# Four image layers on one Trainium2 core: the last layer's depthwise convolution of the first image on VectorE, its diagonals built later, its zeroing divided between two engines

## The chip, the cores and the metric

The program runs on one NeuronCore of a Trainium2 chip. TensorE (PE), VectorE (DVE), ScalarE (ACT), GpSimd (POOL) and SyncE (SP, which only starts DMAs here) each work through a queue of their own in order and wait for one another through semaphores. The metric is the device time of one execution, in microseconds (us). All data are float32.

## The reference

The reference passes 4 images of 192 channels and 56 x 56 pixels through four layers: a windowed attention, a channel gate, another windowed attention with a gated convolution, and a selective scan in four directions. Only the last layer is touched. Cut to what matters, with C = 192 channels, it is:

```python
xn = layer_norm_over_channels(x, ln_w, ln_b)
xc, z = split(in_proj_w @ xn)                       # 192 channels each
xc = silu(depthwise_conv3x3(xc, conv_w) + conv_b)   # 9 weights per channel
for k in range(4):           # rows, columns, and both backwards
    dts, Bv, Cv = split(x_proj_w[k] @ xs[k], [12, 16])
    dt = softplus(dt_proj_w[k] @ dts + dt_proj_b[k])
    h[t] = exp(dt[t] * A) * h[t - 1] + dt[t] * Bv[t] * xs[k][t]   # 4 states per channel
    ys[k][t] = sum(h[t] * Cv[t]) + Ds[k] * xs[k][t]
y = layer_norm_over_channels(sum of the four ys, out_norm_w, out_norm_b) * silu(z)
out = x + out_proj_w @ y
```

## The kernel before, in words

The 192 channels lie as two halves (h = 0, 1) of 96 partitions. Tiles that PE reads have 128 partitions; the 32 that hold no channel are set to zero once. An image has 3136 pixels, worked on in 7 chunks of 448, which are 8 rows of 56.

**Setup of the last layer (L1688 to L1754).** The weights come in by two DMAs (L219). Eight pairs of small matmuls (L1695) work out a projected bias into the PSUM tile `pb`, which DVE copies to `in_b` (L1702). DVE scales the projection weights `inT` by the norm's weights (L1704, one instruction per half) and finishes `a_neg` (L1707). `diag` holds 18 matrices of 96 x 96, one for each half and each of the 9 taps, each an identity times one tap's weight per channel; DVE makes them with 18 `tensor_scalar_mul` (L1722), after POOL has made the identity and zeroed the lower 32 partitions (L1719). The helper `keep` (L1727) allocates tiles and has POOL zero their lower partitions (L1732): two `u` and one `y` of 6272 columns, two `pad` of 1276, four `row` and two `sq` of 896. POOL also zeroes three `dr` (L1740).

**A chunk, `begin(b, c)` (L1792).** SP loads a row tile (L1803). POOL clears the pad's edge columns and copies two rows from the pad above (L1809 to L1815). Then the layer norm: PE averages over channels (L1768), DVE subtracts (L1770), ACT squares (L1778), PE averages (L1783), ACT takes logarithm and exponential (L1786, L1787), DVE multiplies (L1789). PE projects to the first 192 channels (L1821) and ACT writes them into the pad (L1832, one instruction per half). The convolution is on PE: for each half, 9 matmuls of a diagonal with a shifted view of the pad add up in one PSUM bank (L1851; a float32 matmul shows as two instructions), and ACT copies the bank to `u` with the bias (L1859). After each half PE projects one half of z (L1821), which ACT writes to a gate tile (L1868). ACT then applies SiLU to both (L1873, L1874), and `product` (L1887) multiplies `u` by the scan's weights (L1893) and stores the result in memory. When all 7 chunks are there, `begin_columns` does the same product over columns.

**Scans.** A step is one chunk in one direction, a half-step one half of it. It loads the products (`load`), makes dt (L1985, L1997), spreads it by DMA (L2023), takes exponentials (L2031), multiplies dt and u on DVE (L2046 or L2049), spreads this on PE (L2056), multiplies it on DVE (L2062), runs three scans on DVE (L2078), multiplies by C on POOL (L2085), sums on PE (L2101) and adds to `y` on DVE (L2106, L2111, L2115). `final` does the closing norm, the gate and the output projection.

**The order of the work.** `Order` (L241) is a planner that runs while the program is written. Each job is a generator that yields its next operation with an engine and an estimated duration, or a condition that must hold before it goes on. The planner always takes the operation with the smallest (estimated start + 0.05 us x place), and the engines' queues have that order on the chip. Jobs of image 0 have the places -52 + 6c for the chunks, and 2t + h for the scans. A job's next operation is not planned before the one before it has ended. A condition such as `gone("begun", ...)` only orders the plan; on the chip, only data that are written or read make an engine wait.

Of the kernel before, what the change touches and what calls it, by code (L numbers as in the profile page):

```python
# [13 lines left out]
AF = mybir.ActivationFunctionType  # L14
ALU = mybir.AluOpType
# [4 lines left out]
B, C, H, W = 4, 192, 56, 56  # L20
HW = H * W
HALF = 96
CH = 448
# [14 lines left out]
NS, DTR, SCH = 4, 12, 448  # L38
# [176 lines left out]
def load_packs(nc, pool, packs, aps):  # L215
    tiles = {}
    for name, pack in packs.items():
        t = pool.tile([pack.p, pack.n], F32, name=f"w_{name}")
        nc.sync.dma_start(t, aps[name])  # L219
        for n in pack.at:  # L220
            tiles[name + "." + n] = pack.view(t, n)
    return tiles


def pixels(ap):

    return ap.rearrange("(h p) n -> p h n", p=HALF)
# [9 lines left out]
def rows2(ap, w=W):  # L237
    return ap.rearrange("p (y x) -> p y x", x=w)


class Order:  # L241
# [25 lines left out]
    def done(self, tile):  # L267

        (slot,) = (s for slots in self.kinds.values() for s in slots if s[1] is tile)
        slot[0] = self.end + self.LATENCY  # L270
# [58 lines left out]
def on_dve(*n, takes=(), ready=None, each=0.00105):  # L329
    return "DVE", sum(0.08 + each * i for i in n), takes, None, ready  # L330
# [6 lines left out]
def on_act(*n, takes=(), table=None, ready=None):  # L337
    return "ACT", sum(0.2 + 0.0009 * i for i in n), takes, table, ready
# [6 lines left out]
def on_sp(*takes):  # L345
    return "SP", 0.5, takes, None, None
# [1329 lines left out]
def layer3(tc, src, packs, aps, dst):  # L1676
# [7 lines left out]
    nc = tc.nc  # L1684
    with ExitStack() as ctx:
        const = ctx.enter_context(tc.tile_pool(name="c_const", bufs=1))
        dram = ctx.enter_context(tc.tile_pool(name="c_dram", bufs=1, space=DRAM))
        w = load_packs(nc, const, packs, aps)  # L1688
# [25 lines left out]
        nc.vector.memset(eps, EPS)  # L1714

        ident = const.tile([HALF, HALF], F32, name="c_ident")
        make_identity(nc, ident)
        diag = const.tile([128, 2, 9, HALF], F32, name="diag")
        nc.gpsimd.memset(diag[HALF:], 0.0)  # L1719
        for h in range(2):  # L1720
            for t in range(9):
                nc.vector.tensor_scalar_mul(diag[:HALF, h, t], ident, w["c96.conv_w"][:, h, t : t + 1])  # L1722

        per = ctx.enter_context(tc.tile_pool(name="c_per", bufs=1))
        ps = ctx.enter_context(tc.tile_pool(name="c_ps", bufs=1, space=PSUM))

        def keep(name, shape, n, rows=128, zero=True):  # L1727

            tiles = [per.tile([rows, *shape], F32, name=f"{name}{i}") for i in range(n)]
            if zero:  # L1730
                for t in tiles:
                    nc.gpsimd.memset(t[HALF:], 0.0)  # L1732
            return tiles

        us = keep("u", [2, HW], 2)
        (y,) = keep("y", [2, HW], 1)
        pads = keep("pad", [2, 11, W + 2], 2)
        drs = keep("dr", [SCH], 3, zero=False)
        for t in drs:
            nc.gpsimd.memset(t, 0.0)  # L1740
        order = Order(
            nc,
            bank=[ps.tile([128, 512], F32, name=f"c_bank{i}") for i in range(8)],
            row=keep("row", [2, CH], 4),
            sq=keep("sq", [2, CH], 2),
            gate=keep("gate", [2, CH], 2, HALF, False),
            prod=keep("prod", [512], 2, 40, False),
            dr=drs,
            bc=keep("bc", [SCH], 8, zero=False),
            dt=keep("dt", [SCH], 6, HALF, False),  # L1750
            du=keep("du", [SCH], 3, HALF, False),
            da=keep("da", [SCH], 10, zero=False),
            st=keep("st", [SCH], 12, zero=False),
        )  # L1754
        take, done = order.take, order.done
        prods = [[dram.tile([40, HW], F32, name=f"prod{b}_{o}") for o in range(2)] for b in range(B)]
        zmem = [dram.tile([C, HW], F32, name=f"zmem{b}") for b in range(B)]
        passed = set()

        def gone(*what):  # L1760
            return what in passed
# [30 lines left out]
        def begin(b, c):  # L1792


            u = us[b % 2]

            yield lambda: (b, c) == (0, 0) or (gone("begun", b, c - 1) if c else gone("begun", b - 1, NCHUNK - 1))
            yield lambda: b < 2 or gone("scanned", b - 2)

            yield lambda: b == 0 or gone("multiplied", 8 * NSC * (b - 1) + 4 * c)  # L1800
            yield on_sp("row", "row")
            xl, xn = take("row"), take("row")
            nc.sync.dma_start(xl[:HALF], pixels(src[b])[:, :, c * CH : (c + 1) * CH])  # L1803

            i = NCHUNK * b + c
            pad, above = pads[i % 2], pads[(i - 1) % 2]
            yield lambda: i < 2 or gone("convolved", i - 2)
            yield on_pool(200, 200)
            nc.gpsimd.memset(pad[:HALF, :, :, 0 : W + 2 : W + 1], 0.0)  # L1809
            if c == 0:  # L1810
                nc.gpsimd.memset(pad[:HALF, :, 1], 0.0)
            else:
                nc.gpsimd.tensor_copy(pad[:HALF, :, 0:2, 1 : 1 + W], above[:HALF, :, 8:10, 1 : 1 + W])
            if c == NCHUNK - 1:
                nc.gpsimd.memset(pad[:HALF, :, 10], 0.0)  # L1815
            yield from layer_norm(xl, xn, over=(xl,))

            def project(m):
                px = take()
                for k in range(2):  # L1820
                    nc.tensor.matmul(  # L1821
                        px[:HALF, :CH], inT[:, k, HALF * m : HALF * m + HALF], xn[:, k], start=(k == 0), stop=(k == 1)
                    )
                return px

            tiles = []
            for m in range(2):
                yield on_pe(2 * CH, "bank")
                tiles.append(project(m))
            for m in range(2):  # L1830
                yield on_act(CH)
                nc.scalar.activation(  # L1832
                    pad[:HALF, m, 2:10, 1 : 1 + W],
                    rows2(tiles[m][:HALF, :CH]),
                    AF.Identity,
                    bias=in_b[:, m : m + 1],
                )
                done(tiles[m])
            passed.add(("begun", b, c))
            y0, y1 = max(8 * c - 1, 0), 8 * c + (8 if c == NCHUNK - 1 else 7)  # L1840
            n = y1 - y0
            at = y0 - (8 * c - 1)
            px = slice(y0 * W, y1 * W)
            zt = None
            for h in range(2):
                pz = pc = None
                for t in range(9):
                    yield on_pe(n * W, *(("bank",) if t == 0 else ()), ready=order.end - 0.5 if t else None)
                    if t == 0:
                        pc = take()  # L1850
                    nc.tensor.matmul(  # L1851
                        rows2(pc[:HALF, : n * W]),
                        diag[:, h, t],
                        pad[:, h, at + t // 3 : at + t // 3 + n, t % 3 : t % 3 + W],
                        start=(t == 0),
                        stop=(t == 8),
                    )
                yield on_act(n * W)
                nc.scalar.activation(  # L1859
                    u[:HALF, h, px], pc[:HALF, : n * W], AF.Identity, bias=w["c96.conv_b"][:, h : h + 1]  # L1860
                )
                done(pc)
                yield on_pe(2 * CH, "bank")
                pz = project(2 + h)
                yield on_act(CH, takes=() if h else ("gate",))
                if h == 0:
                    zt = take("gate")
                nc.scalar.activation(zt[:, h], pz[:HALF, :CH], AF.Identity, bias=in_b[:, 2 + h : 3 + h])  # L1868
                done(pz)
            done(xn)  # L1870
            passed.add(("convolved", i))
            yield on_act(2 * n * W, 2 * CH, table=SILU)
            nc.scalar.activation(u[:HALF, :, px], u[:HALF, :, px], AF.Silu)  # L1873
            nc.scalar.activation(zt, zt, AF.Silu)  # L1874
            yield on_sp()
            nc.sync.dma_start(pixels(zmem[b])[:, :, c * CH : (c + 1) * CH], zt)
            done(zt)
            yield from product(b, 0, px, u[:, :, px], 2)
            passed.add(("rows", b, c))

        def begin_columns(b, c):
            yield lambda: all(gone("rows", b, i) for i in range(NCHUNK))
# [242 lines left out]
        n = 8 * NSC  # L2125
        for b in range(B):
            for c in range(NCHUNK):
                order.add(n * (b - 1) + 6 * c + 4, begin(b, c))
                order.add(n * (b - 1) + 48 + c, begin_columns(b, c))
                order.add(n * (b + 1) - 2 * c, final(b, c))  # L2130
        for t in range(len(steps)):
            order.add(2 * t - 5, load(t))
            if t % 2 == 0:
                order.add(2 * t - 3, sizes((t, t + 1)))
            for h in range(2):
                order.add(2 * t + h - 1, decay(t, h))
                order.add(2 * t + h, scan(t, h))
# [35 lines left out]
```

## Time and profile before

| | us |
|---|---|
| median of 3 runs | 6957.4 (6956.57 to 6957.86) |
| profiled execution | 6951.71 |
| its span, first to last instruction | 6949.9 |
| PE busy | 5890.7 (85%) |
| DVE busy | 5908.5 (85%) |
| ACT busy | 2640.6 (38%) |
| POOL busy | 1423.8 (20%) |
| mean granted TensorE clock | 0.931 of full speed |

The last layer begins at about 4901 us. Its first real matmul starts at 4926.27 us, the pad of the first chunk is complete at 4943.0, that of the seventh at 5093.5. The first scan of image 0 starts at 5068.9, those of images 1, 2 and 3 at 5585.8, 6061.3 and 6528.2.

In timeline lines, the columns are the start, the time until the last of the merged instructions ends, engine, line, operation, output and inputs with their shapes, the count, and in brackets the idle time before with what ended it. A tile's or line's statistics give the shortest, median and longest duration in ns. An instruction that waits inside its engine for a port has the wait in its duration, not in the idle time before it.

### The profile page before, as it was taken

To read this page: it belongs to the slowest core of one execution; us is meant where nothing else is said; L and a number is where in the kernel's file an instruction comes from. 1 tells how busy PE (TensorE), PEld (TensorE's weight loads), DVE (VectorE), ACT (ScalarE), POOL (GpSimd) and SP (SyncE) were. 2 spreads that over 40 slices of the span, in tenths; PEclk is the share of its full clock that TensorE was granted. 3 is DMA by queue.
4 is the path that set the end of the run, shared out by engine and by line. 5 is a ranking of instruction groups with operands and counts; after the bars stand their busy time and mean duration, and the time that the engine had idled before them with its cause. 6 is when DMAs were issued, how large, how long until landed. Compare 5 with 4: busy or idle time off the path is not lost. (4 is left out here: it accounts for less than half of the span.)

```text
span 6949.9 us, 107660 instructions
## 1 busy us (share of the span) xinstructions
PE 5890.7 (85%) x43810; PEld 2685.0 (39%) x43810; DVE 5908.5 (85%) x7379; ACT 2640.6 (38%) x4083; POOL 1423.8 (20%) x1409
## 2 busy tenths in 40 slices
PE   4999979999999994968888787885799989899776
PEld 2445434444444441345444444442332222222211
DVE  2799999999999999648999898997348788887897
ACT  1111112221122211135555455543256656556543
POOL 0000000000000000032222222220125445445564
PEclk9999989999999997979999899987899999999998
DMA  3222112221222112110000000000145555555654
GB/s 94 56 52 64 34 35 53 58 65 35 52 64 61 35 45 73 45 52 16 19 19 14 19 17 17 19 14 8 34 104 130 142 143 129 152 133 136 166 151 108
DMA packets 252044, 462.69 MB, mean 67 GB/s; under 512 B 30388, under 2 KB 237964, under 8 KB 240412
## 3 DMA queue, kind: packets, MB, share of 16 engines
q1 hardware_dynamic: 251548, 455.80, 25.8%
q8 instruction: 345, 5.65, 0.3%
q14 instruction: 151, 1.24, 0.1%
HBM read 238.58 MB, written 62.96 MB: 43 GB/s over the span
## 5 line engine op out<-in xcount | busy, mean ns | idle before, releaser
L789 DVE TENSOR_TENSOR pr<-vdx,attn 112x1792 f32<-112x1792 f32 (+4 forms) x720 | 1185.6, 1648 | 19.0
L634 PE MATMUL a_bank<-qk_in,w_a 64*49 64x392 f32 x9408 | 1156.3, 496 | 0.0
L2085 POOL TENSOR_TENSOR da<-st,bc 128x448 f32<-128x448 f32 x672 | 859.0, 1283 | 862.9 <-DVE st L2078 618.9
L794 DVE TENSOR_TENSOR oa<-oa,pr 112x1792 f32<-112x1792 f32 (+1 forms) x423 | 764.8, 1808 | 0.0
L634 PE MATMUL a_bank<-qk_in,wd 64*49 64x392 f32 x4032 | 689.6, 493 | 0.0
L2078 DVE TENSOR_TENSOR_SCAN st<-da,st,c_bank 128x448 f32<-128x448 f32 x576 | 646.6, 1132 | 0.0
masks.py:197 POOL MEMSET b_ident<- 128x128 f32 x1 | 0.2, 205 | 2856.0 <-DVE sc L1042 2856.0
L634 PEld LDWEIGHTS a_bank<-qk_in,w_a 64*49 64x49 f32 x9408 | 431.6, 120 | 394.1 <-issue 389.2
L2062 DVE TENSOR_TENSOR c_bank<-c_bank,bc 128x448 f32<-128x448 f32 x672 | 382.5, 618 | 153.1 <-PE c_bank L2056 152.5
L315 ACT ACT_TABLE_LOAD x378 | 485.0, 1283 | 6.6
L2031 ACT ACTIVATE da<-da,a_neg 128x448 f32<-128x448 f32 x672 | 414.1, 658 | 122.5 <-DMA da<-dt 117.9
L1343 DVE SCALAR_TENSOR_TENSOR bg<-bzpad,w_b,bg 128x448 f32<-128x448 f32 (+2 forms) x672 | 423.1, 684 | 0.0
L2101 PE MATMUL c_bank<-da,w_c 128*32 128x448 f32 x1344 | 349.5, 570 | 66.3 <-POOL da L2085 61.4
L1851 PE MATMUL c_bank<-pad,diag 128*96 128x448 f32 (+2 forms) x1008 | 396.8, 543 | 2.4 <-ACT pad L1832 2.3
L794 DVE TENSOR_TENSOR ob<-ob,pr 112x1792 f32<-112x1792 f32 (+3 forms) x282 | 393.0, 1394 | 0.0
L2056 PE MATMUL c_bank<-du,w_c 32*128 32x448 f32 x1344 | 257.8, 624 | 121.6 <-DVE du L2046 80.4
L869 PE MATMUL a_bank<-xc,w_a 128*128 128x448 f32 x672 | 296.8, 571 | 66.0 <-DVE xc L854 66.0
L878 ACT ACTIVATE hm<-a_bank,w_a 128x448 f32<-128x448 f32 x168 | 106.4, 634 | 637.4 <-PE a_bank L869 618.3
L634 PEld LDWEIGHTS a_bank<-qk_in,wd 64*49 64x49 f32 x4032 | 247.4, 119 | 256.5 <-issue 254.6
L1432 PE MATMUL bank<-bxn,w_b 128*128 128x448 f32 (+2 forms) x672 | 288.1, 557 | 24.8 <-DVE bxn L1215 18.6
L884 PE MATMUL a_bank<-hm,w_a 128*96 128x448 f32 x672 | 290.6, 564 | 21.3 <-ACT hm L878 21.3
L655 PE MATMUL a_bank<-qk_sum,w_a 64*49 64x168 f32 (+1 forms) x5376 | 277.7, 337 | 27.1 <-DVE qk_sum L625 25.2
(305 smaller groups left out, 9825.2 us busy)
## 6 DMA issues: line engine op xcount, KB each, us to landing
da<-dt SPq DMA_DIRECT2D x672, 224.0 KB
vdx<-vmem SPq DMA_DIRECT2D x168, 476.0 KB
bc<-prod SPq DMA_DIRECT2D x224, 224.0 KB
row<-x SPq DMA_DIRECT2D x56, 336.0 KB
x<-x SPq DMA_DIRECT2D x4, 2352.0 KB
vmem<-vt SPq DMA_DIRECT2D x56, 168.0 KB
xc<-x SPq DMA_DIRECT2D x56, 168.0 KB
mid<-xc SPq DMA_DIRECT2D x56, 168.0 KB
```

What stands on the lines that cost most here:

```text
L315: self.nc.scalar.preload_act_table_set(table)
L634: nc.tensor.matmul(py[a][outs[g], : 7 * W].rearrange("p (y x) -> p y x", x=W), wt[halves[a], dx], q[halves[a], r, i0 + m : i0 + m + 7, dx ...
L789: nc.vector.tensor_mul(pr, vv, wt)
L794: nc.vector.tensor_add(og, og, before)
L869: nc.tensor.matmul(ph[:, :CH], w["a128.c1T"][:, k, 128 * m : 128 * m + 128], xt[:, k], start=(k == 0), stop=(k == 1),)
L1343: nc.vector.scalar_tensor_tensor(dst, x, wt[:, t : t + 1], dst, ALU.mult, ALU.add)
L1851: nc.tensor.matmul(rows2(pc[:HALF, : n * W]), diag[:, h, t], pad[:, h, at + t // 3 : at + t // 3 + n, t % 3 : t % 3 + W], start=(t == 0), ...
L2031: nc.scalar.activation(da, da, AF.Exp, scale=a_neg[:, k, g : g + 1])
L2062: nc.vector.tensor_mul(tiles[j][:, :SCH], tiles[j][:, :SCH], b_)
L2078: nc.vector.tensor_tensor_scan(sts[j][:, r], da[:, r], tiles[j][:, :SCH][:, r], first, ALU.mult, ALU.add)
L2085: nc.gpsimd.tensor_mul(da, sts[j], c_)
L2101: nc.tensor.matmul(py[32 * j : 32 * j + 32, :SCH], w["c128.sum"], das[j], start=True, stop=True)
```

## The change

The convolution of image 0 is done on DVE: for each half, one `tensor_scalar` (first tap times weight plus bias) and eight `scalar_tensor_tensor`, each of which adds one tap to the rows in `u`. It takes no PSUM bank and no ACT copy. Images 1 to 3 keep the matmuls with diagonals. The diagonals are made by a job of their own, at place 0, on condition that chunk 3 of image 0 is through (`gone("rows", 0, 3)`); the convolutions of the other images are planned after them. `keep` gets the engine that zeroes: DVE for the row, sq and pad tiles, POOL for `u` and `y`. The order of POOL's work becomes `u`, `dr`, the identity, `diag`, `y`. The rest of the diff only adapts calls of `keep`.

```diff
-        make_identity(nc, ident)
         diag = const.tile([128, 2, 9, HALF], F32, name="diag")
-        nc.gpsimd.memset(diag[HALF:], 0.0)
-        for h in range(2):
-            for t in range(9):
-                nc.vector.tensor_scalar_mul(diag[:HALF, h, t], ident, w["c96.conv_w"][:, h, t : t + 1])
...
-        def keep(name, shape, n, rows=128, zero=True):
+        def keep(name, shape, n, rows=128, zero=None):
...
-                    nc.gpsimd.memset(t[HALF:], 0.0)
+                    zero.memset(t[HALF:], 0.0)
...
-        us = keep("u", [2, HW], 2)
-        (y,) = keep("y", [2, HW], 1)
-        pads = keep("pad", [2, 11, W + 2], 2)
-        drs = keep("dr", [SCH], 3, zero=False)
+        rows = keep("row", [2, CH], 4, zero=nc.vector)
+        sqs = keep("sq", [2, CH], 2, zero=nc.vector)
+        pads = keep("pad", [2, 11, W + 2], 2, zero=nc.vector)
+        us = keep("u", [2, HW], 2, zero=nc.gpsimd)
+        drs = keep("dr", [SCH], 3)
         for t in drs:
             nc.gpsimd.memset(t, 0.0)
+        make_identity(nc, ident)
+        nc.gpsimd.memset(diag[HALF:], 0.0)
+        (y,) = keep("y", [2, HW], 1, zero=nc.gpsimd)
...
-                pz = pc = None
-                for t in range(9):
+                pz = pc = uh = None
+                if b == 0:
+                    for t in range(9):
+                        yield on_dve(n * W, each=0.0012, ready=order.end - 0.3 if t else None)
+                        v = pad[:HALF, h, at + t // 3 : at + t // 3 + n, t % 3 : t % 3 + W]
+                        uh = rows2(u[:HALF, h, px])
+                        wt = w["c96.conv_w"][:, h, t : t + 1]
+                        if t == 0:
+                            nc.vector.tensor_scalar(uh, v, wt, w["c96.conv_b"][:, h : h + 1], ALU.mult, ALU.add)
+                        else:
+                            nc.vector.scalar_tensor_tensor(uh, v, wt, uh, ALU.mult, ALU.add)
+                if uh is None:
+                    yield lambda: gone("diagonals")
+                for t in range(9 if uh is None else 0):
                     yield on_pe(n * W, *(("bank",) if t == 0 else ()), ready=order.end - 0.5 if t else None)
...
-                yield on_act(n * W)
-                nc.scalar.activation(
-                    u[:HALF, h, px], pc[:HALF, : n * W], AF.Identity, bias=w["c96.conv_b"][:, h : h + 1]
-                )
-                done(pc)
+                if uh is None:
+                    yield on_act(n * W)
+                    nc.scalar.activation(
+                        u[:HALF, h, px], pc[:HALF, : n * W], AF.Identity, bias=w["c96.conv_b"][:, h : h + 1]
+                    )
+                    done(pc)
...
+        def diagonals():
+            yield lambda: gone("rows", 0, 3)
+            for h in range(2):
+                for t in range(9):
+                    yield on_dve(HALF)
+                    nc.vector.tensor_scalar_mul(diag[:HALF, h, t], ident, w["c96.conv_w"][:, h, t : t + 1])
+            passed.add(("diagonals",))
...
+        order.add(0, diagonals())
```

## The prediction

> **What bounds the kernel now.** I first read the busy shares by stretch of time, to find the stage that the edits touch, then the timeline of DVE, POOL and PE in the two stretches that matter, then the waits. The edits touch the head of the last layer. Its columns are: stretch, length, busy us of PE, of the weight loads, of DVE, ACT and POOL with counts, granted clock, DMA share, GB/s.
>
> ```profile
> 4900.00:4950.00 50.00, 22.56 (x60) 10.58 (x59) 27.11 (x30) 6.71 (x9) 28.16 (x21) 0.66 0.18 50
> 4950.00:5000.00 50.00, 48.69 (x131) 20.04 (x130) 4.79 (x5) 19.57 (x27) 1.05 (x4) 1.00 0.11 31
> 5000.00:5050.00 50.00, 48.70 (x130) 19.28 (x128) 4.28 (x5) 23.39 (x31) 1.05 (x4) 1.00 0.24 62
> 5050.00:5100.00 50.00, 50.00 (x144) 19.62 (x143) 15.34 (x19) 30.40 (x44) 7.68 (x11) 1.00 0.36 94
> ```
>
> Two different limits stand in these rows. Until about 4943 PE waits while DVE and POOL prepare. From there to about 5154 PE is full (48.7 to 50.0 of 50 us) and DVE is nearly idle (4 to 15 of 50). The timeline shows what the preparation is:
>
> ```profile
> 4904.06 21.04 DVE L1722 TENSOR_SCALAR diag<-c_ident,w_c 96x96 f32<-96x96 f32 x18
> 4925.03 1.07 DVE L1704 TENSOR_SCALAR w_c<-w_c,w_c 96x384 f32<-96x384 f32 x1
> 4926.03 0.14 DVE L1702 COPY in_b<-pb 96x4 f32<-96x4 f32 x1
> ```
> ```profile
> 4904.00 10.70 POOL L1732 MEMSET u<- 32x6272 f32 x2 [0.52 <-DMA w_c<-c]
> 4914.65 5.43 POOL L1732 MEMSET y<- 32x6272 f32 x1
> 4924.15 3.74 POOL L1732 MEMSET row<- 32x896 f32 x4
> ```
> ```profile
> 4926.27 3.27 PE L1768 MATMUL c_bank<-row,c_ones 128*96 128x448 f32 x4 [13.25 <-issue]
> ```
>
> PE's first real matmul (L1768) starts at 4926.27, 0.10 us after the copy L1702 ends; pb and the first bank take turns in PSUM, so I take that copy as its releaser (row 0 was zeroed by 4925.0). The copy is behind L1704, and L1704 behind 18 diagonals. These are slow for a reason that the durations give:
>
> ```profile
> L1722 DVE TENSOR_SCALAR diag<-c_ident,w_c x18: 425/1119/5406, 4904.1 to 4924.3; 96x96 f32<-96x96 f32 x18
> ```
>
> The longest, 5.406 us for 96 elements, end within 0.1 us of the ends of POOL's 5.4 us memsets: two diagonals pass per memset. So a tensor_scalar of SBUF data waits here for a POOL memset; a DVE memset does not (c_ones took 0.138 us at 4901.64 inside POOL's diag memset). The Trainium skill, SBUF — State Buffer, section Who interferes with whom, says the same of such operations, an exclusive lock.
>
> In the full stretch, per chunk of image 0, PE does 36 conv matmuls (two halves, 6.93 us plus 6.22 and 0.99), 14.0 of a period of 25.3 us.
>
> **Sum, part 1: the start.** Removed from DVE before L1704: 18 diagonals (21.04). Added on DVE: eight memsets. DVE's own memsets give 0.138 us for 96 elements and 0.218 for 192, so about 0.8 us for 896 (six) and 1.1 for 1276 (two): 7 us (7.8 at POOL's rows, 0.94 and 1.24), from about 4904 to 4912. L1704 is then next, but it overwrites what the pb matmuls read until 4913.02 (10.33 plus 2.69), and it must pass POOL's memset: two u from 4904.0 end at 4914.7. So L1704 and L1702 end near 4914.8, and L1768 starts near 4914.5 instead of 4926.3: **12 us**. If u starts 2.4 us earlier the lock is passed at 4913.3: 13. If one more 5.4 us memset gets in front: 6.5. The second L1704 and L1707 pass behind the 0.5 us dr memsets and end by 4916.5, before L1770 needs DVE. POOL then does dr 1.5, identity 0.4, diag 1.5, y 5.4: to 4923.8, and the pad edges L1809 to 4924.4. The first reader of the pad comes at 4930.8, so y and diag hide there; without that cover they cost up to what they run over. SP's order does not change; the first two row loads (issued 4903.9 and 4904.2) fall in a DMA burst that is over by 4911.5.
>
> **Part 2: the chunks of image 0.** Removed per chunk: 36 PE matmuls and two ACT copies of 0.63. Added on DVE: two times one tensor_scalar (0.43 from start to start) and eight scalar_tensor_tensor. The nearest row is layer 2's convolution of the same shape:
>
> ```profile
> L1343 DVE SCALAR_TENSOR_TENSOR bxn<-bapad,w_b,bxn x448: 606/672/1195, 3107.9 to 4824.1; 96x448 f32<-96x448 f32 x106, 96x392 f32<-96x392 f32 x22, 96x504 f32<-96x504 f32 x22
> ```
>
> 0.672 each, 0.595 from start to start, so a half is 5.2 us. There, two tiles alternate; here each reads what the last wrote. Sums that follow their product at once (L794 behind L789) start 0.09 before its end, so I keep 0.595; held until the end plus 0.07, the gap between the three L1341 from 4759.56, it would be 0.74. The new path from one pad to the next, with DVE in the order half, subtraction, half, product, since the planner prefers the older chunk: 5.2, 1.0, 5.2, 1.1, then four projections and two ACT writes 3.9: 16.4. Meanwhile square, variance and logarithm (3.6 to 5.2) hide under the second half. Two additions: PE now has gaps of 2 to 4 us, and the trace shows the granted clock halved after 1.98 us without work (L1783 at 5122.93, 3.21 us instead of 1.74), so a cold projection adds up to 1.8; and SiLU with its table (1.28, 0.95, 0.93) may stand between the two ACT writes, up to 3.1. I take 18.5 (16.4 to 21.3). The Trainium skill (TensorE: Matmul & The Clock Gate, HAM oscillation) warns of gaps above about 3.4 us; by that rule alone most gaps here would stay warm and the period be near 16.4, 8 us more over the chunks, but the 1.98 us gap of this trace speaks for the colder value.
>
> From the fifth chunk on, a scan half-step joins: on DVE 0.6, 1.69, three of 1.06 and 0.68, together 6.2; POOL's three products share the lock. DVE then has 10.6, 2.1 and 6.2, or 19; I take 22 (20 to 25) against 26.5. Pads were finished at 4943.0, 4964.7, 4989.9, 5015.1, 5040.4, 5067.0, 5093.5: six periods of together 150.5. After: four of 18.5 and two of 22, 118: **32.5** (15.5 to 45). The last chunk, from its pad to its SiLU, took 26.6; now 5.8, 1, 5.8, 6.2 and some 5 for what is behind, 24: **3** (0 to 5).
>
> **Part 3: what comes back.** The diagonals run on DVE after chunk 3. If they fall in the gap of 4 to 6 us between product and next pad, they cost 0; if every pair waits for a POOL product of 1.13 us, 18 cost 11. I take **-3**. The only new wait is PE's first convolution of image 1 for them; behind it in PE's queue stand the scans' matmuls, but it comes after 5118, where L1768 of image 1 ran, some 60 us behind chunk 3. POOL's pad edges now wait for DVE's last read in place of PE's, one chunk ahead of need. Half-steps done when the columns begin (three before 5130): from there to the end 221 half-steps take 1820 us, 8.2 each; half of one lost, **-4** (+8 to -16). The rest of the layer is the same work, shifted. Planner noise: first scans of images 1, 2, 3 are 475.5 and 466.8 apart, so some 5 us either way.
>
> Sum 12 + 32.5 + 3 - 3 - 4 = 40.5. The profiled execution took 6951.7 (span 6949.9), 5.7 under the median of the runs; 6951.7 - 40.5 = 6911.2, and on the median of 6957.4 it is **6917**. Own range 6894 to 6942.
>
> **Rivals.** (a) **Only the start is gained.** DVE with convolution, norm and scan, the halved clock and SiLU's place keep the period near 25, so the 32.5 goes, and diagonals or lag take 3 to 12 of the 12: 6948 to 6957, no change. For: PE's gaps. Against: DVE has 4.3 of 50 us busy there, and 10.6 per 25 us fit. 15%. (b) **Slower: DVE becomes the bound in the chunks.** Mechanism: the convolution's operations have two SBUF inputs and meet POOL's products, which read SBUF. The trace has such meetings: POOL's product takes 1.75 instead of 1.13 behind L2049 (5270.33), and 21 of 112 L2046 took longer than 0.64, up to 2.60 us. The point is 0.93 us per operation, where 18 of them, 2.1 and 6.2 make 25. At 1.195, the slowest in the row, a chunk needs 29.8: seven times 4.5 is 32 slower, with diagonals 11, less the 12 of the start: 6988. Against: POOL has products in the last three chunks only. The section of the Trainium skill named above says that two-input operations contend with GpSimd's reads and not with its writes; the two rows agree for reads. 8%. (c) **More than forecast:** no SiLU between, a warm PE, periods of 16.4 and 20, one half-step more: 13 + 45 + 5 + 8 = 71, 6886. 7%. That the change does not do what it says: the diagonals merely move; it is the -11 in (a).
>
> **Chances.** Forecast 70%, (a) 15, (b) 8, (c) 7. About 0.2%, 14 us, can be told from no change. Faster than 6943.5: forecast and (c) less 1, 76%. Same: (a) and some of the forecast's tail, 16%. Slower: (b), 8%. The range 6888 to 6956 leaves out (b), most of (c) and the end of (a).
>
> **What would show it.** L1768's start near 4914.5; L1704 ending with a POOL memset. Pads of image 0 some 18.5 us apart, then 22; PE near two thirds busy from 4931 to 5053, with half clocks; the DVE operations 0.6 apart. The columns' products (5129.8 before) near 5083. First scan of image 1 (5585.8) some 40 earlier, and that distance kept to the end. Wrong if the pads are 24 or more apart, if the diagonals stand in front of a scan that PE waits for, or if the distance at image 1 is gone by image 3.

## The result and the profile after

The changed kernel takes 6903.9 us (median of 6 runs, 6901.5 to 6912.1) against 6957.6 us before (6 runs, 6952.7 to 6960.5): a ratio of 0.9925, 95% interval 0.9912 to 0.9938. That is 53.8 us less; the prediction said 40.5 less, 6917 us, with a range of 6888 to 6956.

The layers ahead are untouched, but they do not take the same time in each execution: in the 14 profiles of this study the last layer begins at 4901.3 to 4914.8 us. So from here on, times of the last layer are counted from the end of DVE's last instruction of the layer before (L1514). In the two first profiles, in us (the gains are taken before rounding):

| | before | after | gained by then |
|---|---|---|---|
| first matmul of the norm (L1768) | 24.9 | 11.0 | 13.9 |
| first subtraction of the norm (L1770) | 28.2 | 24.1 | 4.2 |
| pad of the first chunk complete | 41.6 | 35.8 | 5.8 |
| pad of the seventh chunk | 192.2 | 149.8 | 42.4 |
| first columns' product | 228.4 | 181.3 | 47.1 |
| first scan of image 1 | 684.5 | 630.4 | 54.0 |
| end | 2048.6 | 1994.6 | 54.0 |

After image 0 the gain stays within 0.4 us. The busy shares by stretch (same columns as in the prediction) show the exchange that the change makes, PE from 49 to 50 of 50 us down to 36 to 39, DVE from 4 to 15 up to 38 to 44, and, as its price, a granted clock of 0.86 to 0.89 where it was 1.00:

```profile
4950.00:5000.00 50.00, 38.68 (x84) 13.64 (x82) 37.93 (x56) 24.76 (x33) 1.81 (x6) 0.89 0.20 56
5000.00:5050.00 50.00, 38.19 (x92) 12.57 (x93) 43.71 (x68) 33.55 (x47) 5.30 (x8) 0.86 0.44 116
5050.00:5100.00 50.00, 36.18 (x84) 9.16 (x83) 42.22 (x62) 24.73 (x34) 15.05 (x14) 0.86 0.33 88
```

One period of DVE in the changed kernel, from the timeline. It is the order that the prediction named, half, subtraction, half, product, and then DVE waits 3.05 us for the pad:

```profile
4977.00 0.51 DVE L1855 TENSOR_SCALAR u<-pad,w_c 96x448 f32<-96x448 f32 x1 [3.22 <-ACT pad L1832]
4977.55 5.70 DVE L1857 SCALAR_TENSOR_TENSOR u<-pad,w_c,u 96x448 f32<-96x448 f32 x8
4983.17 1.07 DVE L1770 TENSOR_TENSOR row<-row,c_bank 96x896 f32<-96x896 f32 x1
4984.16 0.50 DVE L1855 TENSOR_SCALAR u<-pad,w_c 96x448 f32<-96x448 f32 x1
4984.70 5.70 DVE L1857 SCALAR_TENSOR_TENSOR u<-pad,w_c,u 96x448 f32<-96x448 f32 x8
4990.32 1.07 DVE L1789 TENSOR_TENSOR row<-row,c_bank 96x896 f32<-96x896 f32 x1
4994.44 0.51 DVE L1855 TENSOR_SCALAR u<-pad,w_c 96x448 f32<-96x448 f32 x1 [3.05 <-ACT pad L1832]
```

In every period ACT's SiLU comes ahead of the first write into the pad, which follows it without a gap:

```profile
4992.89 0.93 ACT L1888 ACTIVATE gate<-gate 96x896 f32<-96x896 f32 x1
4993.73 0.61 ACT L1832 ACTIVATE pad<-c_bank,in_b 96x448 f32<-96x448 f32 x1
```

And the start. First DVE, then POOL, from the changed kernel's timeline:

```profile
4917.64 0.16 DVE L1702 COPY in_b<-pb 96x4 f32<-96x4 f32 x1 [4.05 <-PE pb L1695]
4917.72 3.29 DVE L1704 TENSOR_SCALAR w_c<-w_c,w_c 96x384 f32<-96x384 f32 x2
4921.24 0.81 DVE L1727 MEMSET sq<- 32x896 f32 x1 [0.22 <-issue]
4922.06 5.19 DVE L1707 TENSOR_SCALAR a_neg<-a_neg 128x24 f32<-128x24 f32 x1
4927.47 0.81 DVE L1727 MEMSET sq<- 32x896 f32 x1 [0.22 <-issue]
4928.49 1.12 DVE L1727 MEMSET pad<- 32x1276 f32 x1 [0.22 <-issue]
4929.83 1.12 DVE L1727 MEMSET pad<- 32x1276 f32 x1 [0.21 <-issue]
4930.98 1.08 DVE L1770 TENSOR_TENSOR row<-row,c_bank 96x896 f32<-96x896 f32 x1
```
```profile
4906.98 0.17 POOL masks.py:197 MEMSET c_ident<- 96x96 f32 x1 [8.59 <-DVE bp L1514]
4907.20 1.53 POOL L1739 MEMSET diag<- 32x1728 f32 x1
4908.81 0.26 POOL masks.py:199 TENSOR_SCALAR_AFFINE_SELECT c_ident<-c_ident 96x96 f32<-96x96 f32 x1
4909.60 10.58 POOL L1727 MEMSET u<- 32x6272 f32 x2 [0.53 <-DMA w_c<-c]
4920.24 1.60 POOL L1737 MEMSET dr<- 128x448 f32 x3
4921.89 5.32 POOL L1727 MEMSET y<- 32x6272 f32 x1
```

L1702 releases PE's first matmul early, as hoped. But the sign of a_neg, 24 elements, takes 5.19 us: it was taken up 0.17 us after POOL had begun to zero y, and it ends 0.04 us after that memset. On the chip the identity and the zeroing of diag came ahead of u, not between dr and y as in the program, so y follows dr at once. Four memsets of DVE were laid around it in the queue (one ahead of it, three behind), and the subtraction, whose mean was ready at 4921.2, stands behind all of them until 4930.98. The wait that the change took away came back on the same engine, through the same lock.

### The profile page after: what moved, and what is told of

It is laid out like the page before. It is cut to its first block, busy times and chain, and to the rows that moved or that the text cites. A ratio compares the mean times of both kernels' runs of the same rounds, so it can differ in the third digit from the quotient of the medians.

```text
span 6901.5 us, 107266 instructions
## 1 busy us (share of the span) xinstructions
PE 5804.0 (84%) x43558; PEld 2646.9 (38%) x43558; DVE 5990.2 (87%) x7513; ACT 2632.0 (38%) x4071; POOL 1409.7 (20%) x1401
## 4 chain that ended last, share of the span: by engine, by line
DVE 47%; PE 38%; issue 7%; ACT 4%; POOL 2%; DMA 2%; SPq 0%; DVEq 0%; POOLq 0%; ACTq 0%
DVE pr L789 9%; DVE oa L794 6%; PE a_bank L634 6%; DVE bg L1343 5%; DVE ob L794 4%; PE c_bank L1864 4%; DVE bxn L1343 3%; DVE st L2101 3%; PE a_bank L869 2%; PE a_bank L884 2%; PE c_bank L2079 2%; PE c_bank L1821 2%; PE c_bank L2124 2%; DVE c_bank L2085 2%; PE c_bank L1952 2%
## 5 line engine op out<-in xcount | busy, mean ns | idle before, releaser
L1432 PE MATMUL bank<-bxn,w_b 128*128 128x448 f32 (+2 forms) x672 | 293.6, 566 | 23.7 <-DVE bxn L1215 17.8
L586 ACT ACTIVATE qk_in<-a_bank,qk_bias,qk_scale 64x224 f32<-64x224 f32 (+5 forms) x288 | 146.1, 525 | 407.5 <-PE a_bank L571 405.1
L655 PE MATMUL a_bank<-qk_sum,w_a 64*49 64x224 f32 (+1 forms) x5376 | 275.6, 336 | 30.2 <-DVE qk_sum L625 28.3
```

## The experiments

My theory after the result: the convolution on DVE frees PE in the chunks of image 0 (36.6 us in the six periods, 4.6 in the last chunk), the start gives only 5.8 because of the lock, and the remaining 7.0 us, between the columns' products and image 1, need a cause, as the instructions of DVE, ACT and POOL have the same order there in both kernels, but for one scan and one exponential in the first 11 us.

**1. The zeroing alone.** The changed kernel with

```diff
-                if b == 0:
+                if b < 0:
...
-        order.add(0, diagonals())
```

and the identity, the zeroing of diag and the 18 diagonals back in their old place.

> The zeroing shared by DVE and POOL as in the change, but the convolution of image 0 stays on PE and the diagonals are built in the setup, as before. My theory: the change's gain comes from the chunks of image 0, where PE was full; with the convolution on PE their pads stay 25.3 us apart (26.5 for the last two). The start gains little or loses, because the 18 diagonals, each pair behind a POOL memset, still stand before the scaling of the projection weights and DVE has some 7 us of memsets more: 6950 to 6965 us. Rival, that the zeroing is the gain: about 6910 to 6925.

Measured: 6956.0 us against 6958.1 (ratio 0.9998, 0.9989 to 1.0007): no change. The periods are those of before, 21.8 and then 25.1 to 26.5; the first pad is complete at 44.8, later than before (41.6). DVE's timeline of this kernel shows that the diagonals still take 17.8 us behind POOL and that the memsets then delay the subtraction; the sign of a_neg meets no memset here, and takes 0.18 us:

```profile
4918.48 17.83 DVE L1722 TENSOR_SCALAR diag<-c_ident,w_c 96x96 f32<-96x96 f32 x18
4936.23 0.15 DVE L1702 COPY in_b<-pb 96x4 f32<-96x4 f32 x1
...
4938.07 0.18 DVE L1707 TENSOR_SCALAR a_neg<-a_neg 128x24 f32<-128x24 f32 x1
```

**2. The convolution alone.** The reverse: DVE convolves image 0, the setup is that of before. Shown against the kernel before:

```diff
-                for t in range(9):
+                if b == 0:
+                    for t in range(9):
+                        yield on_dve(n * W, each=0.0012, ready=order.end - 0.3 if t else None)
...
+                for t in range(9 if uh is None else 0):
```

> The convolution of image 0 on DVE as in the change, but all zeroing on POOL and the diagonals in the setup, as before. My theory: the start stays as before (first pad 41.6 us after the last instruction of DVE in the layer before, against 35.8 in the changed kernel), the pads are 17 to 18 us apart in the first chunks and 20 to 22 in the last two, and the end comes 36 plus 5 us, perhaps 7 more, sooner than before: 6908 to 6917 us. Rival, that the start must be shortened as well for the chunks to gain: above 6930.

Measured: 6911.0 us (ratio 0.9933, 0.9920 to 0.9945). First pad at 41.8, periods 15.3, 18.0, 18.3, 19.1, 21.6, 21.9, columns at 183.1. So at the columns the convolution alone has gained 45.3 of the 47.1 us of the whole change. The shorter start, 5.9 us ahead in the changed kernel, is still there at the seventh pad (149.8 against 156.0), though its first period is longer (17.0 against 15.3). Of this lead some 4.5 us go in the last chunk (31.6 against 27.0 from the pad to the columns), where some of the diagonals stand. Of the 10.2 us by which run 2 ends later than the changed kernel, only 1.7 are there at the columns.

**3. Without the diagonals.** The job at place 0 does nothing, and diag is zeroed whole, so images 1 to 3 get the bias alone from their convolution.

```diff
-        nc.gpsimd.memset(diag[HALF:], 0.0)
+        nc.gpsimd.memset(diag, 0.0)
...
-                for t in range(9):
-                    yield on_dve(HALF)
-                    nc.vector.tensor_scalar_mul(diag[:HALF, h, t], ident, w["c96.conv_w"][:, h, t : t + 1])
+                pass
```

> The changed kernel without its 18 diagonal instructions: diag is zeroed instead, so the convolutions of images 1 to 3 give only the bias; the work of all engines otherwise stays. My theory: in the changed kernel most diagonals take 0.17 us of DVE between other work in the fifth and sixth chunk and two of them 1.1 us behind a POOL product, so that they cost 2 to 5 us there: 6899 to 6902 us, periods of the fifth and sixth chunk 1 to 2 us shorter. Rival, that they are hidden in DVE's gaps: no difference, 6904.

Measured: 6907.4 us (ratio 0.9923, 0.9910 to 0.9935), no gain over the change. But the columns start at 175.6, 5.7 us sooner: the sixth period is 20.0 instead of 21.9, and the last chunk is 3.8 shorter. The diagonals do cost 5.7 us; 6.5 were then lost again before image 1, where this kernel takes 455.6 us and the changed one 449.1. So what is won in the chunks does not reach the end one for one, and this run made the 7 us more pressing.

**4. The victim of the lock removed.**

```diff
-        nc.vector.tensor_scalar_mul(a_neg, a_neg, -1.0)
+        nc.scalar.activation(a_neg, a_neg, AF.Identity, scale=-1.0)
```

> The changed kernel, but the sign of a_neg is turned by ACT instead of a tensor_scalar on DVE. My theory: in the changed kernel that instruction waits 5.2 us for POOL's memset of y, and the first subtraction of the norm stands behind it; without it the first subtraction starts some 5.3 us sooner (some 18.8 us after the last DVE instruction of the layer before, against 24.1) and the end comes as much sooner: 6898 to 6899 us. Rival, that the memsets of sq and pad or the pad's edges on POOL set the start anyway: 6903 to 6904.

Measured: the first subtraction at 18.8 us, as expected, the first pad at 32.2 (35.8), the end at 1990.8 (1994.6), 3.8 us sooner. DVE's timeline:

```profile
4914.34 3.13 DVE L1704 TENSOR_SCALAR w_c<-w_c,w_c 96x384 f32<-96x384 f32 x2
4917.69 1.75 DVE L1727 MEMSET sq<- 32x896 f32 x2 [0.23 <-issue]
4919.65 1.12 DVE L1727 MEMSET pad<- 32x1276 f32 x1 [0.21 <-issue]
4920.99 1.12 DVE L1727 MEMSET pad<- 32x1276 f32 x1 [0.21 <-issue]
4922.15 1.08 DVE L1770 TENSOR_TENSOR row<-row,c_bank 96x896 f32<-96x896 f32 x1
```

The runs do not separate it from the change: median 6904.2 of 6894.7 to 6905.7, ratio 0.9919 (0.9905 to 0.9932).

**5. The holder of the lock moved.** POOL zeroes y in a job after the pad of chunk 1.

```diff
-        (y,) = keep("y", [2, HW], 1, zero=nc.gpsimd)
+        (y,) = keep("y", [2, HW], 1)
...
+        def clear_y():
+            yield lambda: gone("begun", 0, 1)
+            yield on_pool(2 * HW, each=0.00085)
+            nc.gpsimd.memset(y[HALF:], 0.0)
...
+        order.add(0, clear_y())
```

> The changed kernel, but POOL zeroes y by a job of the planner after the pad of chunk 1, and the sign of a_neg stays on DVE. My theory: what held the sign, and behind it the first subtraction, was POOL's memset of y and not the instruction's own place; with the holder gone instead of the victim, the first subtraction starts near 18.9 us after the last DVE instruction of the layer before (18.8 with the sign on ACT, 24.1 in the changed kernel), and the first pad is at 32 instead of 35.8. Time 6895 to 6905 us. Rival, that the sign's own place in DVE's queue counts: 24 us and no gain. In the convolution of chunk 1 or 2 one tensor_scalar may now wait up to 5.4 us for the memset of y.

Measured: the subtraction at 19.2, the first pad at 32.5: victim or holder, the gain is the same, so it is the lock. But 6913.7 us (ratio 0.9934, 0.9921 to 0.9948): the second period is 23.8 instead of 18.0. The lock, which I had feared, is not the reason there: the memset ran at 4940.2, before that period. The norm's subtraction stands behind both halves there (4968.23) instead of between them. I put this down to the planner, which reckons 5.3 us of POOL ahead of the next pad's edges and so plans the next norm later; this was not shown by a run. At the columns this kernel is only 1.4 us behind the changed one. The larger part of the 10.5 us by which it ends later comes in the stretch behind them, 458.6 us instead of 449.1.

**6. The norm first.** The part of begin from the convolution on becomes a job of its own with a later place for image 0.

```diff
...
+        for c in range(NCHUNK):
+            order.add(6 * c - n + 20, convolve_first(c))
```

> The changed kernel, but the convolutions of image 0 are jobs of their own with a later place, so that the planner puts the norm of the next chunk between the convolution's operations instead of after its halves. My theory: the periods of 17 to 18 us are set by a chain (half, subtraction, half, product, projection, ACT), not by DVE's throughput (12.9 + 2.1 = 15.0 us per chunk); with the norm earlier the projection lies beside the second half and the first four periods fall to 15 to 16 us, some 10 us in all: 6890 to 6900 us. Rival, that DVE or PE is the bound there: periods unchanged, 6904.

Measured: 6912.1 us (ratio 0.9932, 0.9920 to 0.9945); the expectation was wrong. Periods 19.2, 17.1, 17.1, 17.1, 16.9, 21.8. One period of DVE:

```profile
4972.78 0.51 DVE L1856 TENSOR_SCALAR u<-pad,w_c 96x448 f32<-96x448 f32 x1 [2.88 <-ACT pad L1832]
...
4978.94 1.08 DVE L1770 TENSOR_TENSOR row<-row,c_bank 96x896 f32<-96x896 f32 x1
...
4984.66 1.07 DVE L1789 TENSOR_TENSOR row<-row,c_bank 96x896 f32<-96x896 f32 x1
...
4989.92 0.51 DVE L1856 TENSOR_SCALAR u<-pad,w_c 96x448 f32<-96x448 f32 x1 [2.88 <-ACT pad L1832]
```

The product now stands inside the second half, but the subtraction still comes after a half, and the chain is half, subtraction to product, product to the next half: 6.2, 5.7 and 5.3 us. DVE and PE both have room (41.1 and 42.2 us busy in three periods, which last 51.3 us); the chain is the limit, and half of the convolution stays in it. The chunks did gain, 4.8 us by the seventh pad and 2.1 by the columns, but the stretch to image 1, where the order of work is another one, is the longest of all, 462.2 us.

**7. Past the point of turning.** The convolution of image 0 is done twice.

```diff
-                    for t in range(9):
+                    for t in [*range(9), *range(9)]:
```

> The changed kernel, but the convolution of image 0 is done twice in place (36 operations per chunk instead of 18, the second pass writes the same result again), to put DVE over the point at which the prediction saw the change turn slower. By the predicted point (0.93 us for each of 18 operations; here two times 0.715, so 1.43) and 7 chunks: 18 x 0.50 x 7 = 63 us over no gain in the chunks, 6985 to 7010 us, slower than before; the first four periods 30 us, the last two 32 to 36. Rival, that DVE has room for it: 6930 to 6950.

Measured: 6997.1 us, ratio 1.0053 (1.0040 to 1.0066), slower than before. Periods 30.4 to 31.0, the last two 32.9 and 34.9. The operation's own duration (the median, 681 ns) is that of the changed kernel; from one start to the next it is 0.717 us in both:

```profile
L1857 DVE SCALAR_TENSOR_TENSOR u<-pad,w_c,u x224: 621/681/1433, 4941.0 to 5163.0; 96x448 f32<-96x448 f32 x80, 96x392 f32<-96x392 f32 x16, 96x504 f32<-96x504 f32 x16
```

**8 and 9. A short start, with the norm first and without.** The sign on ACT, sq and pad zeroed by POOL ahead of all else, u and y in pieces later; run 8 has the norm first as well.

```diff
-        sqs = keep("sq", [2, CH], 2, zero=nc.vector)
-        pads = keep("pad", [2, 11, W + 2], 2, zero=nc.vector)
-        us = keep("u", [2, HW], 2, zero=nc.gpsimd)
+        sqs = keep("sq", [2, CH], 2, zero=nc.gpsimd)
+        pads = keep("pad", [2, 11, W + 2], 2, zero=nc.gpsimd)
+        us = keep("u", [2, HW], 2)
...
-        (y,) = keep("y", [2, HW], 1, zero=nc.gpsimd)
+        (y,) = keep("y", [2, HW], 1)
...
+        def clear(t, c):
+            yield lambda: gone("begun", 0, c)
+            for k in range(8):
+                yield on_pool(784, each=0.00085)
+                nc.gpsimd.memset(t[HALF:, :, 392 * k : 392 * k + 392], 0.0)
...
+        order.add(-52, clear(us[0], 0))
+        order.add(0, clear(us[1], 1))
+        order.add(0, clear(y, 2))
```

> The changed kernel with the norm first as in the run above, the sign of a_neg on ACT, the sq and pad tiles zeroed by POOL ahead of everything large, and u and y zeroed by POOL in pieces of 784 columns (0.7 us) after the first pads. My theory: DVE then meets no long memset, the first subtraction follows the first mean at once, 14 to 15 us after the last DVE instruction of the layer before (24.1 in the changed kernel), and the chunks gain some 10 us: 6878 to 6892 us. Rival, that something else holds the start (the weights' landing, the pieces of u in front of the convolution): no better than the sign on ACT, 6895 to 6904.

Measured: the subtraction at 14.0, the first pad at 27.5, the columns at 169.5, 11.9 us ahead of the changed kernel; but 6904.1 us (ratio 0.9921, 0.9907 to 0.9934), and an end at 1994.3, as in the change (1994.6). All 11.9 us went between the columns and image 1: 461.5 us instead of 449.1, with the order of work of run 6.

> The changed kernel with the short start of the run above (sign of a_neg on ACT, sq and pad zeroed by POOL first, u and y zeroed by POOL in pieces after the first pads), but the planner's order of norm and convolution as in the change. My theory: the first subtraction stands at 14 to 15 us after the last DVE instruction of the layer before, the first pad at 27 to 28 (35.8 in the changed kernel), the periods as in the changed kernel within 1 us, so the columns' products start 6 to 8 us sooner; the stretch from there to the first scan of image 1 takes 449 to 459 us, by the time PE spends at half clock in it. 6891 to 6906 us, 6896 if that stretch is the short one. Rival, that the order of the later work changes as it did with the norm first and gives it back: 6903 to 6912.

Measured: 6899.4 us (6899.2 to 6905.5; ratio 0.9917, 0.9903 to 0.9930), the lowest median of all, end at 1990.9. Its interval overlaps with the change's. The subtraction is at 14.6 and the first pad at 28.1, but the second pad takes 22.4 instead of 17.0; as in run 5, the subtraction stands behind both halves there. The rest of the periods (within 0.7 us) and the stretch to image 1, 449.1, are those of the change.

**10 to 12. Both kernels again.** Unchanged, for the 7 us.

> The kernel before, profiled once more. In the two first profiles the stretch from the columns' products to the first scan of image 1 took 456.1 us before and 449.1 after, with the same order of instructions there and 34 against 14 us at half clock. My theory: these 7 us depend on the half-clock time of the execution, so that executions of one kernel differ; stretch = 449 + 0.35 x (half-clock us - 14) within 1 us. The chunks' periods repeat within 0.3 us. Rival, that the 7 us belong to the change: 456 here again with 34 us.

> The changed kernel, profiled once more, for the same question. My theory: the stretch lies anywhere in 449 to 459 us, on the line 449 + 0.35 x (half-clock us - 14). Rival, that the short stretch belongs to the change: 449 again.

> The changed kernel, profiled a third time, for the same question and with the same expectations: on the line anywhere in 449 to 459 us, or, by the rival, 449 again.

Measured: 456.1 us again before, with 34.1 us at half clock; 449.1 and 449.1 after, with 13.7 and 13.7; 6956.8, 6899.9 and 6901.5 us. One half of my theory fell: the stretch is no luck of the execution but repeats to 0.1 us in both kernels. The rival stood, at least in that the short stretch comes with this kernel. The other half, the line 449 + 0.35 x (half-clock us - 14), held, and it holds within 0.8 us for all kernels of the table below.

What it goes with is the granted clock all the same. The rows of that stretch for the kernel before, the changed one, run 2 and run 7, from the busy shares, with the clock in the column behind POOL:

```profile
5129.72:5585.80 456.08, 417.13 (x1323) 125.27 (x1322) 351.57 (x455) 269.15 (x388) 211.89 (x174) 0.96 0.54 136
```
```profile
5088.30:5537.40 449.10, 408.17 (x1323) 123.23 (x1322) 351.04 (x455) 269.91 (x388) 212.05 (x174) 0.98 0.55 137
```
```profile
5087.50:5545.80 458.30, 418.92 (x1325) 125.67 (x1322) 352.05 (x454) 270.19 (x388) 212.34 (x175) 0.96 0.54 134
```
```profile
5176.20:5625.20 449.00, 408.04 (x1323) 123.13 (x1322) 350.91 (x454) 269.95 (x388) 212.07 (x174) 0.98 0.54 137
```

The work of DVE, ACT and POOL agrees within 1.1 us; PE is busy 408 us in the short stretches and 417 to 419 in the long ones. In the trace's clock record the half-clock time comes in multiples of 3.41 us. Counting where in this raster of 3.41 us the columns' products begin sorts the kernels that have the changed kernel's order of work there, or that of before, so that neighbours have like times:

| kernel | begin in the raster | us at half clock | stretch |
|---|---|---|---|
| run 1 | 0.05 | 27.3 | 454.1 |
| before, twice | 0.34, 0.40 | 34.1 | 456.1 |
| after, three times; runs 4, 9 | 0.87 to 0.93 | 13.7 | 449.1 |
| run 7 | 1.12 | 13.7 | 449.0 |
| run 3 | 2.00 | 30.7 | 455.6 |
| run 5 | 2.32 | 41.0 | 458.6 |
| run 2 | 2.60 | 41.0 | 458.4 |

Run 7 starts the columns 89 us later than the changed kernel and has the same stretch, at nearly the same place in the raster; run 2 starts them 1.7 us later and takes 9.3 us more. So the 7 us go with where the columns happen to fall, not with work that the change removed.

The traces hold a second test. From the first scan of image 1 to that of image 2, and from there to that of image 3, all four engines do the same work in the same order, in every kernel (up to four matmul records at the ends). That gives 28 stretches of equal work. Counted in the same raster, the 13 that begin at 0.16 to 0.19 take 466.8 to 466.9 us, with 27.3 us at half clock; the 14 that begin at 2.50 to 2.89 take 475.2 to 475.5, with 51.2; one, of run 7, begins at 2.99 and takes 470.6, with 41.0. In run 1 the short one is image 1's and in the kernel before image 2's. So neither the image nor the kernel sets the time, and the place goes with it here too. It is still a tie: a run that moves the place alone was not made, and how the clock is decided is left open.

## Why the prediction was right, and where not

- **What bounds the kernel** was right: PE in the chunks, the diagonals behind POOL's memsets at the start. Runs 1 and 2 separate the two: the convolution alone brings 45.3 us by the columns, the zeroing alone nothing. Rival (a), a period that stays near 25, fell with the periods of 15.3 to 21.9 in run 2.
- **The start: 12 predicted, 5.8 measured.** The step that failed: "The second L1704 and L1707 pass behind the 0.5 us dr memsets and end by 4916.5, before L1770 needs DVE." L1768 was even earlier than said (11.0 after the layer's begin; predicted 13.2, though L1702, which it follows, was put at 13.5). But L1707 met y, not dr, since the identity and the zeroing of diag, which I had put between the two, had run ahead of u. And I had taken all eight memsets of DVE to be done before the weights land; four ran afterwards. Without the lock (run 4) 5.3 us of the subtraction's delay are gone, and with neither the four memsets nor a long memset of POOL ahead of it (runs 8, 9) it stands at 14.0 to 14.6.
- **The periods: 32.5 predicted, 36.6 measured** (150.5 to 113.9; predicted 118). Some of the diagonals run in them, which the prediction counts as a term of their own; without the diagonals (run 3) it is 38.5. The sum was nearly right through errors that cancel. The operations are 0.717 us apart, not 0.595: the row that I had named and put aside, 0.74 for one that waits for the last one's result, was nearly the true one, 1.0 us more per half. On the other side, of the 2.1 us put on top of the chain little came. The first half needs only the first of the two pad writes, so the second projection lies beside it. The cold PE was there (L1783 takes 3.27 us after 3.39 without work) but lies under the second half. SiLU did not come between the writes but ahead of the first, which waited 0.5 us for it in the period shown (its projection ended at 4993.19).
- The Trainium skill's warning of gaps above about 3.4 us (TensorE: Matmul & The Clock Gate, HAM oscillation) does not hold the other way. In run 6 three projections after 2.99 us without work start at half clock and take 7.71 us, against 4.67 in the kernel before (both rows below), and a gap of 1.98 us did it in the kernel before.

```profile
4985.79 7.71 PE L1821 MATMUL c_bank<-row,w_c 128*96 128x448 f32 x12 [2.99 <-DVE row L1789]
```
```profile
4984.51 4.67 PE L1821 MATMUL c_bank<-row,w_c 128*96 128x448 f32 x12
```

- **The last chunk: 3 predicted, 4.6 measured,** and 8.5 without the diagonals that run in it (run 3).
- **The diagonals: -3 predicted, -5.7 measured** at the columns (run 3), already inside the 36.6 and 4.6 above. Most take 0.17 us from one start to the next, two wait 1.1 us behind a POOL product; the convolution's queue simply leaves them no gap.
- **By the columns** these terms add up to 44.5 predicted and 47.1 measured. That they lie so close is in good part luck. The gain at the start was put 6.2 us too high, those of the periods and the last chunk without diagonals 6.0 and 5.5 too low, and the loss to the diagonals 2.7 too low.
- **The lag of the scans: -4 predicted, none measured**: four half-steps have begun when the columns start, in both kernels. This step was mis-sized, with what follows.
- **After the columns: nothing predicted but a shift, 7.0 more measured**, which goes with the time at half clock (table above). This is the largest part of the 13 us by which the forecast was too small; 7.0 lies within the lag's bound of +8, but the reason is another one.
- **Rival (b)**, slower when an operation costs more than 0.93 us: run 7 puts 1.43 in its place and is 0.53% slower, 6997 where the formula gave 6985 to 7010. The rival was right in its point and wrong for this kernel, which stays at 0.717.

## What to carry to other kernels

Before moving work to an idle engine, write down the chain that the moved work will stand in, not only the two engines' loads: here the engine had room and the chain still set the period, also when the order was changed. A short DVE operation that can be locked out by a long POOL memset belongs before it, on another engine, or next to memsets cut in pieces; look for what else is queued behind it. And when a gain of several us appears in a stretch that the change does not touch, profile both kernels again and compare the granted clock before giving it to the change.

## What the runs showed of the hardware that was not expected

With nearly the same order of instructions, image 0's remaining work took 449.0 to 458.6 us, with 13.7 to 41.0 us at half clock, and repeated to 0.1 us in the two kernels that were profiled more than once. Images 1 and 2, with the same order, took 466.8 to 475.5. Both times go with where the work begins within a raster of 3.41 us, and the difference is more than the 18 diagonals cost.
